# Scores in bursts of three head pairs, with a shared exponential, in a graph attention stack

## Chip, cores and metric

One core of a Trainium2 chip runs the whole program. The metric is the device time of one execution in microseconds. A core has five engines that run beside one another and wait for each other by semaphores: TensorE (PE; its weight loads are listed as PEld), VectorE (DVE), ScalarE (ACT), GpSimd (POOL) and SyncE (SP, which issues the DMAs here). Matmuls write PSUM, which has 8 banks of 128 partitions x 512 float32.

## What is computed

Sixteen graphs of 1024 nodes with 128 features share one adjacency matrix. Each goes through three transformer layers with masked attention, and then through one graph attention layer:

```python
# layers 0, 1, 2 (8 heads of 16)
Q, K, V = h @ Wq, h @ Wk, h @ Wv              # split into heads
scores = einsum('bnhd,bmhd->bhnm', Q, K) / sqrt(16)
scores = where(adj == 0, -inf, scores)
attn = softmax(scores, axis=-1)
x = layer_norm(h + einsum('bhnm,bmhd->bnhd', attn, V) @ Wo + bo)
x = layer_norm(x + relu(x @ W1 + b1) @ W2 + b2)
# layer 3
h = x @ W;  s_i = h @ a_src;  s_j = h @ a_dst
e = leaky_relu(s_i[:, :, None] + s_j[:, None, :], 0.2)
att = softmax(where(adj == 0, -inf, e))
out = layer_norm(einsum('bij,bjd->bid', att, h) + x)
```

Everything is float32. The softmax runs without subtracting a maximum; sums come from a column of ones beside V, and a check of their range at the end chooses a general path that isn't taken here.

## The kernel before

**Blocks and steps.** A block is one layer of one graph: 16 x 3 = 48 blocks, ordered in groups of four graphs (`blocks`). A block has 32 steps `(m, g, qh, kt)`: head group g (the heads are taken as four of each of two groups), half of the queries qh (512), tile of 128 keys kt. A step covers four heads, which are two pairs (`pp` 0 and 1).

**Scores** (`score_step`, L415 to L437). For each pair two matmuls with 64-row operands (L423, the rows hold high and low parts of q or k) fill a PSUM `slot()` of two banks; there are three slots, tag `s`. A pair is masked in one of two ways. On POOL: ACT takes the exponential from PSUM into the step's tile `e` (L430) and POOL multiplies by a 0/1 mask in place (L431). On DVE: DVE adds 0 or -57344 while it moves the scores from PSUM to `e` (L433), and ACT takes the exponential in place later (`exponentials`, L445). Pair 0 goes to POOL except at kt 2, 5 and 7 (`BOTH_ON_DVE`); pair 1 goes to DVE always. The 0/1 mask `mask01` has two bytes an element, the added one `mask_add` one byte.

**Products** (`av_step`, L447). Four steps later (`AHEAD`) eight matmul instructions multiply the four heads' exponentials by V into the accumulator bank `acc` (L450), 32 columns of the array for each head. After eight key tiles `finish` (L461 to L464) transposes the accumulator on DVE and divides.

**Pieces.** Everything else is cut into tasks that a planner puts between the steps: `piece()` runs at most one due task of the `chains` after each step's products. `AT` and `AT_END` give a step within the block for each task of `proj` (transposes, k and q with their high and low parts, v; L357 to L397) and `post` (output projection, norms, feed-forward; L469 to L529). `need()` forces a task that must be done. The last layer's tasks (`last_tasks`) follow gaps instead. A piece's matmuls use the one bank `t` (`bank()`), and ACT or DVE empties it. `split` casts the bank to the high part on ACT (L385) and subtracts it on DVE (L386). `edges(u)` makes 1024 x 256 edge weights: for each of two slots four matmuls (L607) and one DVE operation with `mask01` (L610), into a tile of the `e` pool; `aggregate(u)` multiplies them by the node features. `two(f, g)` runs an edge task and an aggregation as one piece.

**Stacking.** `stack(m, g)` copies the high and low parts of k and q into 64-row form, with 16 DMAs from SP for each group (L408). Group 1 is put down at step 1 of the block, and the next block's group 0 at step 21, after `need(("proj", m + 1))`.

**Order.** PE and ACT follow program order (`manual_schedule`). DVE and POOL follow the planner of the language, where `soon()` raises a priority, except at the start. Steps 1 to 4 also build the masks of the last four adjacency rows (`FIRST`).

**Tiles.** The `e` pool has 6 tiles of 128 x 4 x 512 float32; at the start they hold the first adjacency rows too.

Of the kernel before, what the change touches and what calls it, by code (L numbers as in the profile page):

```python
# [12 lines left out]
I32 = mybir.dt.int32  # L13
# [14 lines left out]
NEG_SLOPE = 0.2  # L28
SOON = 120
LANES = 4  # L30
FIRST = 1


AT = {"proj": (3, 6, 9, 11, 14, 15, 19, 20), "post": (12, 22, 23, 25, 26, 27, 28, 30, 32, 40, 41)}
AT_END = {3: (12, 21, 22, 24, 25, 26, 27, 28, 30, 31), 2: (8, 9, 13, 14, 15, 16, 17, 18, 20, 21)}
AHEAD = 4
BOTH_ON_DVE = (2, 5, 7)
TILES = {"w": 10, "x": LANES + 1, "last": 2}
BLOCKED = -57344.0

# [75 lines left out]
def fast_path(ctx: ExitStack, tc: tile.TileContext, a: dict, out: bass.AP, flag):  # L116
# [13 lines left out]
    def slot(dtype=F32):  # L130

        return psum.tile([P, N], dtype, tag="s", name="s", bufs=3)

    def bank():

        if head[0] or tail[0]:
            return slot()[:, :512]
        return psum.tile([P, 512], F32, tag="t", name="t", bufs=1)
# [5 lines left out]
        return work.tile([P, 512], F32, tag="w", name=name, bufs=TILES["w"])  # L144

    def e_tile():
        return work.tile([P, J, 512], F32, tag="e", name="e", bufs=6)


    def load_x(b):  # L150
# [25 lines left out]
    chk = const.tile([P, 2, B * (L + 1)], F32)  # L176


    mask01 = const.tile([P, NT, N], BF16)
    mask_add = const.tile([P, NT, N], F8W)  # L180
    rows_in = []
    for t in range(NT):
        if t < 6:
            ai = work.tile([P, 2, N], I32, tag="e", name="ai", bufs=6)
            ai, ab = ai[:, 0], ai.bitcast(BF16)[:, 1, :N]
        else:
            ai = work.tile([P, N], I32, tag="Wk", name="ai", bufs=4)
            ab = work.tile([P, N], BF16, tag="Wq", name="ab", bufs=4)
        rows_in.append((ai, ab))
# [15 lines left out]

    def masks(t, ps):
        psv = ps.rearrange("p (k q) -> p k q", q=P)
        nc.vector.tensor_copy(mask01[:, :, t * P:(t + 1) * P], psv)
        nc.scalar.activation(mask_add[:, :, t * P:(t + 1) * P], psv, AF.Identity, scale=-BLOCKED, bias=blocked,
                             saturate=False)  # L210

# [13 lines left out]
    def first_weights():  # L225
        W[0].update(load_layer(nc, nc.sync, const, a, 0, ("Wo", "b2", "W1", "b1", "W2", "ln1_g", "ln2_g")))
        norm_weights(nc.sync, 0)
# [184 lines left out]

    def score_step(step):  # L415
        m, g, qh, kt = step
        e = e_tile()
        q0 = qh * 512
        for pp in range(2):
            q, k = state["Wq", g, pp], state["Wk", g, pp]  # L420
            ps = slot()
            for r in range(2):
                nc.tensor.matmul(ps[:, r * 512:(r + 1) * 512], k[64 * r:64 * r + 64, kt * P:(kt + 1) * P],  # L423
                                 q[64 * r:64 * r + 64, q0:q0 + 512], start=True, stop=True)
            ev = e[:, 2 * pp:2 * pp + 2, :]
            psv = ps.rearrange("p (r q) -> p r q", q=512)
            on_pool = pp == 0 and kt not in BOTH_ON_DVE
            m = (mask01 if on_pool else mask_add)[:, kt, q0:q0 + 512][:, None, :].to_broadcast([P, 2, 512])
            if on_pool:
                nc.scalar.activation(ev, psv, AF.Exp, scale=HD ** -0.5)  # L430
                behind["pool"] = nc.gpsimd.tensor_mul(ev, ev, m).ins  # L431
            else:
                behind["dve"] = nc.vector.tensor_add(ev, psv, m).ins  # L433
                masked.append((2 * step_no[0] + pp + (kt not in BOTH_ON_DVE), ev))
        step_no[0] += 1
        exponentials()
        return e  # L437

    masked, step_no = [], [0]

    def exponentials(n=None):

        while masked and (n is not None or masked[0][0] < 2 * step_no[0] - 1):
            _, ev = masked.pop(0)
            nc.scalar.activation(ev, ev, AF.Exp, scale=HD ** -0.5)  # L445

    def av_step(step, e, acc, first, last):  # L447
        m, g, qh, kt = step
        for j in range(J):
            nc.tensor.matmul(acc[j * SLOT:j * SLOT + HD + 1, :], v_bufs[m % 2][:, kt, 2 * j + g, :], e[:, j, :],  # L450
                             start=first, stop=last)

    def finish(g, qh, acc):

# [80 lines left out]

    g_rows = const.tile([P, N], F32R)
    h_rows = const.tile([P, 512], F32R)

    def last_tasks(b):
# [54 lines left out]


        def edges(u):
            def run():
                e = s["e", u] = e_tile().rearrange("p j (c q) -> p (j c) q", q=256)  # L600
                for c in range(2):

                    ps = slot()
                    for i in range(2):
                        for r in range(2):
                            row = slice(64 * r + g0, 64 * r + g0 + 4)
                            nc.tensor.matmul(ps[:, (2 * r + i) * 256:(2 * r + i + 1) * 256],  # L607
                                             h_rows[row, (2 * i + c) * P:(2 * i + c + 1) * P],
                                             g_rows[row, u * 256:(u + 1) * 256], start=True, stop=True)
                    nc.vector.scalar_tensor_tensor(e[:, c:NT:2, :], ps.rearrange("p (j q) -> p j q", q=256), 1.0,  # L610
                                                   mask01[:, c:NT:2, u * 256:(u + 1) * 256], op0=OP.max, op1=OP.mult)
            return run

        def aggregate(u):
            def run():
                e, ps = s["e", u], bank()
                for i in range(2):
                    for t in range(NT):
# [21 lines left out]

        def two(f, g):
            def run():
                f()
                g()
            return run

        return [(5, xt(0), "+w +last +w +w"), (1, xt(1), "+w"), (2, nodes(0, 3), ""), (2, nodes(3, 6), ""), (2, nodes(6, 8), "-w -w"),
# [78 lines left out]

    def av_due(n):

        for item in [w for w in waiting if w[2] <= n]:
            step, e, _ = item  # L730
            half = step[:3]
            if half not in accs:
                if accs:
# [2 lines left out]
                left[half] = NT  # L736
            waiting.remove(item)
            left[half] -= 1
            av_step(step, e, accs[half], left[half] == NT - 1, left[half] == 0)
            if left[half]:  # L740
                continue
            m, g, qh = half
# [16 lines left out]
                if l == L - 1:  # L759
                    put(last_tasks(b), ("last", b), chain)  # L760

    n = 0
    with tc.manual_schedule(engines={mybir.EngineType.PE, mybir.EngineType.Activation}):
        for m, (b, l) in enumerate(blocks):
            order = [(g, qh) for g in range(G) for qh in range(2)]
            if m in (0, len(blocks) - 1):
                order.sort(key=lambda x: x[1])
            for at, (g, qh, kt) in enumerate((g, qh, kt) for g, qh in order for kt in range(NT)):
                now[0] = n
                if at == (6 if m == 0 else 1):  # L770
                    stack(m, 1)
                if n == 6:
                    with tc.issue_after(behind["stack"]):
                        first_weights()
                        other_weights()
                if n == 20:
                    with tc.issue_after(behind["pool"]):
                        biases()
                if n == 40:
                    with tc.issue_after(behind["dve"]):  # L780
                        last_weights()
                if at == 0 and m + 2 < len(blocks) and blocks[m + 2][1] == 0:
                    put([(0, fetch(blocks[m + 2][0]), "+x")], ("fetch", blocks[m + 2][0]))
                if m + 1 < len(blocks):
                    if at == (6 if m == 0 else 0):
                        need(("post",) + (blocks[m + 1][0], blocks[m + 1][1] - 1) if blocks[m + 1][1] else
                             ("fetch", blocks[m + 1][0]))
                        put(proj_tasks(m + 1), ("proj", m + 1), first=True)
                    if at == (24 if m == 0 else 21):
                        need(("proj", m + 1))  # L790
                        stack(m + 1, 0)
                step = m, g, qh, kt
                if FIRST <= n < FIRST + 4:

                    with tc.manual_schedule(engines={mybir.EngineType.DVE}):
                        e = score_step(step)
                        neighbours(4 + n - FIRST)
                        masks(4 + n - FIRST, mask_rows(4 + n - FIRST))
                else:
                    e = score_step(step)  # L800
                waiting.append((step, e, n + AHEAD))
                av_due(n)
                piece()
                n += 1
        exponentials(0)
        for n in range(n, n + 2 * AHEAD):
            now[0] = n
            av_due(n)
            piece()
        tail[0] = True  # L810
        while chains:
            now[0] += 1
            for chain in list(chains):
                if is_due(chain):
                    take(chain)
# [236 lines left out]
```

## Time and profile before

| | us |
|---|---|
| median of 3 runs (lowest, highest) | 3996.08 (3995.59, 3997.26) |
| the profiled execution | 3992.41 |
| its span, first to last instruction | 3990.6 |
| ACT exponentials from PSUM, L430, x960 | 983.6 busy, 1025 ns each |
| PE products, L450, x12288 | 1632.5 busy, 603 ns each |
| PE scores, L423, x6144 | 1175.0 busy, 455 ns each |
| DVE edge operation, L610, x128 | 150.3 busy, 1213 ns each |
| POOL layer norm scale, L345, 128x1024, x95 | 227.5 busy, 2395 ns each |

The mean granted TensorE clock is 0.985. A group's busy time is the union of its instructions' spans. Matmuls overlap, so on PE the distance from start to start says more than the duration; on ACT and DVE, too, an instruction starts some 0.1 us before its predecessor's span ends. The last column of a group's line is the idle time of the engine before it, and what ended most of it. In the timeline, consecutive instructions of one line are merged.

### The profile page before, as it was taken

The numbers are of one execution on the slowest core, as the hardware profiler recorded it, in microseconds if no ns is written. First come the engines' busy times: TensorE is split into PE (matmuls) and PEld (weight loads), VectorE is DVE, ScalarE is ACT, GpSimd is POOL, SyncE is SP. The second block draws the span as 40 slices with busy tenths as digits, with TensorE's granted clock in tenths as the row PEclk, the third lists the DMA queues.
The fourth block names the chain that finished last, engine by engine and source line by source line (L and its number), as shares of the span: only waits on it lengthen the run. The fifth ranks groups of instructions, "written<-read, shape, count | busy, mean of one in ns | idle before, by whom it ended". The sixth has DMA issues, their size and how long they took to land.

```text
span 3990.6 us, 107765 instructions
## 1 busy us (share of the span) xinstructions
PE 3758.4 (94%) x44501; PEld 1550.6 (39%) x44501; DVE 3410.8 (85%) x5326; ACT 3380.6 (85%) x3961; POOL 3454.8 (87%) x3010
## 2 busy tenths in 40 slices
PE   7999999999999999999999999999999999999996
PEld 2333333344443333334444333333444433333345
DVE  7888988988888988988788898888888898898874
ACT  7999999977779999997777999999777799999860
POOL 5889989988889999998888998999888898998975
PEclk8999999999999999999999999999999999999998
DMA  6222222112222222222222222221222212222200
GB/s 162 64 65 55 53 65 65 48 44 75 55 55 52 65 65 55 53 65 55 55 55 55 65 57 52 65 65 46 57 52 55 65 48 65 64 52 56 65 8 20
DMA packets 124464, 233.12 MB, mean 58 GB/s; under 512 B 34624, under 2 KB 73792, under 8 KB 123968
## 3 DMA queue, kind: packets, MB, share of 16 engines
q1 hardware_dynamic: 123056, 225.74, 22.6%
q8 instruction: 354, 5.80, 0.6%
q14 instruction: 142, 1.16, 0.1%
q10 hardware_dynamic: 912, 0.42, 0.0%
HBM read 15.54 MB, written 8.39 MB: 6 GB/s over the span
## 4 chain that ended last, share of the span: by engine, by line
PE 60%; DVE 18%; POOL 14%; issue 4%; ACT 3%; SPq 0%; DMA 0%; DVEq 0%; POOLq 0%; ACTq 0%
PE acc L450 23%; PE t L297 18%; PE s L423 15%; DVE e L433 10%; POOL e L431 7%; POOL x L345 3%; POOL x L346 3%; DVE st L322 3%; PE t L286 2%; DVE x L329 1%; POOL mv L339 1%; ACT e L445 1%; DVE lo L386 1%; PE s L297 1%; DVE mv L324 1%
## 5 line engine op out<-in xcount | busy, mean ns | idle before, releaser
L433 DVE TENSOR_TENSOR e<-s,mask_add 128x1024 f32<-128x1024 f32 x2112 | 2492.2, 1213 | 320.0 <-PE s L423 242.8
L445 ACT ACTIVATE e<-e 128x1024 f32<-128x1024 f32 x2112 | 2194.3, 1062 | 197.0 <-DVE e L433 181.8
L431 POOL TENSOR_TENSOR e<-e,mask 128x1024 f32<-128x1024 f32 x960 | 2055.1, 2155 | 326.3 <-ACT e L430 306.2
L450 PE MATMUL acc<-e,v 128*17 128x512 f32 x12288 | 1632.5, 603 | 56.4 <-POOL e L431 25.2
L423 PE MATMUL s<-Wq,Wk 64*128 64x512 f32 x6144 | 1175.0, 455 | 52.3 <-DVE e L433 35.1
L430 ACT ACTIVATE e<-s 128x1024 f32<-128x1024 f32 x960 | 983.6, 1025 | 241.6 <-PE s L423 241.5
L423 PEld LDWEIGHTS s<-Wq,Wk 64*128 64x128 f32 x6144 | 498.9, 185 | 1009.6 <-issue 396.2
L450 PEld LDWEIGHTS acc<-e,v 128*17 128x17 f32 x12288 | 208.0, 95 | 565.6 <-issue 464.4
L341 POOL TENSOR_SCALAR x<-x,mv 128x128 f32<-128x128 f32 x896 | 392.0, 453 | 23.5
L339 POOL TENSOR_TENSOR mv<-mv,half_neg 128x4 f32<-128x4 f32 x224 | 232.7, 1039 | 18.7
L345 POOL TENSOR_TENSOR x<-x,ln_g 128x1024 f32<-128x1024 f32 (+1 forms) x97 | 230.0, 2372 | 11.7 <-PE t L286 6.1
L297 PE MATMUL t<-hd,e 128*32 128x129 f32 x7040 | 207.8, 275 | 1.2
L329 DVE TENSOR_TENSOR x<-t,x 128x512 f32<-128x512 f32 x191 | 130.8, 685 | 85.6 <-PE t L297 85.6
L322 DVE BATCH_NORM_STATS2 st<-x 128x6 f32<-128x128 f32 x896 | 197.2, 279 | 3.3
L297 PEld LDWEIGHTS t<-hd,e 128*32 128x32 f32 x7040 | 193.5, 110 | 16.7 <-DVE lo L386 9.9
L297 PE MATMUL t<-x1T,W 128*32 128x512 f32 x1520 | 198.0, 592 | 0.0
L297 PEld LDWEIGHTS t<-W,hT 128*32 128x32 f32 x6080 | 169.9, 110 | 58.5 <-issue 45.2
L297 PE MATMUL t<-W,hT 128*32 128x128 f32 x6080 | 183.4, 273 | 0.2 <-DVE x L625 0.2
L286 PEld LDWEIGHTS t<-identf,x 128*128 128x128 f32 x872 | 93.8, 141 | 221.7 <-issue 81.8
L286 PE MATMUL t<-identf,x 128*128 128x128 f32 x872 | 153.7, 291 | 21.7 <-DVE hd L575 7.1
L386 DVE TENSOR_TENSOR lo<-t,hi 128x512 fp32r<-128x512 f32 x188 | 128.2, 682 | 35.6 <-ACT hi L385 35.6
L610 DVE SCALAR_TENSOR_TENSOR e<-s,mask 128x1024 f32<-128x1024 f32 x128 | 150.3, 1213 | 6.1 <-PE s L607 5.4
(118 smaller groups left out, 2493.9 us busy)
## 6 DMA issues: line engine op xcount, KB each, us to landing
Wk<-hi SPq DMA_DIRECT2D x384, 128.0 KB
Wk<-lo SPq DMA_DIRECT2D x384, 128.0 KB
Wq<-hi SPq DMA_DIRECT2D x384, 128.0 KB
Wq<-lo SPq DMA_DIRECT2D x384, 128.0 KB
x<-in_x_dram SPq DMA_DIRECT2D x16, 512.0 KB
out_dram<-x SPq DMA_DIRECT2D x31, 256.0 KB
ai<-in_adj_dram SPq DMA_DIRECT2D x8, 512.0 KB
g_rows<-parts SPq DMA_DIRECT2D x124, 4.0 KB
```

Of the source, the lines that this page charges most:

```text
L286: nc.tensor.transpose(ps[:, t * P:(t + 1) * P], src[:, 4 * h + t, :], identf)
L297: nc.tensor.matmul(dst[j:j + SLOT, :], lhsT[:, j:j + SLOT], rhs, start=start, stop=stop)
L322: nc.vector.bn_stats(st[:, t, :], z[:, t, :])
L339: nc.gpsimd.tensor_tensor(v, v, half_neg[:, ts], OP.pow)
L341: nc.gpsimd.tensor_scalar(z[:, t, :], z[:, t, :], mv[:, t, 0:1], mv[:, t, 1:2], op0=OP.add, op1=OP.mult)
L345: nc.gpsimd.tensor_mul(z, z, rows(gain, n))
L423: nc.tensor.matmul(ps[:, r * 512:(r + 1) * 512], k[64 * r:64 * r + 64, kt * P:(kt + 1) * P], q[64 * r:64 * r + 64, q0:q0 + 512], start=Tru ...
L430: nc.scalar.activation(ev, psv, AF.Exp, scale=HD ** -0.5)
L431: behind["pool"] = nc.gpsimd.tensor_mul(ev, ev, m).ins
L433: behind["dve"] = nc.vector.tensor_add(ev, psv, m).ins
L445: nc.scalar.activation(ev, ev, AF.Exp, scale=HD ** -0.5)
L450: nc.tensor.matmul(acc[j * SLOT:j * SLOT + HD + 1, :], v_bufs[m % 2][:, kt, 2 * j + g, :], e[:, j, :], start=first, stop=last)
```

## The change

- Scores are issued in bursts of three pairs, that is one and a half steps, whatever step a pair belongs to. In a burst, pairs 1 and 3 are masked on DVE into the two halves of one `e` tile, and pair 2 on POOL into a tile of a new pool `ep`. In every 16th burst pair 2 goes to DVE too. The DVE pairs of a burst share one exponential of 128 x 2048, which ACT runs in the next burst.
- After a burst's scores come the products and pieces of the steps that it completed, one or two in turn. Where it completed two, the exponentials come first, then products, piece, products, piece. Where one or none, a piece comes first, then the exponentials, then products and a piece.
- An edge task no longer computes at once: it queues its fill, and the next burst is the fill and one pair, on POOL. `two` runs the aggregation first.
- `mask01` has one byte an element. The `e` pool has 5 tiles, `ep` 4 of 128 x 2 x 512.
- The second q piece of `proj` moves from step 15 to 17.
- The masks of the last four rows are built in the first four bursts.

```diff
-FIRST = 1
-AT = {"proj": (3, 6, 9, 11, 14, 15, 19, 20), "post": (12, 22, 23, 25, 26, 27, 28, 30, 32, 40, 41)}
+AT = {"proj": (3, 6, 9, 11, 14, 17, 19, 20), "post": (12, 22, 23, 25, 26, 27, 28, 30, 32, 40, 41)}
-BOTH_ON_DVE = (2, 5, 7)
+BURST = 3
+POOL_RESTS = 16
+E_TILES = {"e": 5, "ep": 4}
...
-    mask01 = const.tile([P, NT, N], BF16)
+    mask01 = const.tile([P, NT, N], F8W)
...
+    def on_dve(step, pp, ev):
+        psv = scores(step, pp)
+        behind["dve"] = nc.vector.tensor_add(ev, psv, mask_of(mask_add, step)).ins
+        e_of.setdefault(step, {})[pp] = ev
+
+    def on_pool(step, pp, ev):
+        psv = scores(step, pp)
+        nc.scalar.activation(ev, psv, AF.Exp, scale=HD ** -0.5)
+        behind["pool"] = nc.gpsimd.tensor_mul(ev, ev, mask_of(mask01, step)).ins
+        e_of.setdefault(step, {})[pp] = ev
+
+    e_of, masked, bursts = {}, [], [0]
+
+    def burst(edge, pairs):
+        old = list(masked)
+        masked.clear()
+        if edge is not None:
+            edge()
+            on_pool(*pairs[0], e_pair())
+        else:
+            e, ep = e_tile(), e_pair()
+            rests = bursts[0] % POOL_RESTS == POOL_RESTS - 1 or len(pairs) < BURST
+            for i, pair in enumerate(pairs):
+                if i == 1:
+                    (on_dve if rests else on_pool)(*pair, ep)
+                else:
+                    on_dve(*pair, e[:, i:i + 2, :])
+            masked.append(e[:, 0:2 * ((len(pairs) + 1) // 2)])
+            if rests and len(pairs) > 1:
+                masked.append(ep)
+            bursts[0] += 1
+        return old
+
+    def exponentials(evs):
+        for ev in evs:
             nc.scalar.activation(ev, ev, AF.Exp, scale=HD ** -0.5)
...
+            def run():
+                extra.append(fill)
+                if tail[0]:
+                    flush()
             return run
 
         def aggregate(u):
             def run():
+                if ("e", u) not in s:
+                    flush()
...
+        while p < 2 * len(steps):
+            edge = extra.popleft() if extra else None
+            take_n = 1 if edge else min(BURST, 2 * len(steps) - p)
+            pairs = []
+            for i in range(p, p + take_n):
+                if i % 2 == 0:
+                    before(i // 2)
+                pairs.append((steps[i // 2], i % 2))
...
+            p += take_n
+            ready = range(full, p // 2)
+            full = p // 2
+            for n in ready:
+                waiting.append((steps[n], n + AHEAD))
+            if len(ready) == 2:
+                exponentials(old)
+                av_due(ready[0])
+                at_step(ready[0], piece)
+                av_due(ready[1])
+                at_step(ready[1], piece)
+            else:
+                n = p // 2 - 1
+                at_step(n, piece)
+                exponentials(old)
+                if ready:
+                    av_due(n)
+                    at_step(n, piece)
```

`scores(step, pp)` holds the two matmuls and the slot of the old `score_step`, `mask_of` the broadcast slice of a mask, and `before(n)` the stacking, loads and task entries that the old loop ran ahead of a step. `av_step` takes each pair's exponentials from where its burst put them.

More of the change, by code (lines that the diff above doesn't have):

```diff
@@ L146, in e_tile, with e_pair @@
     def e_tile():
-        return work.tile([P, J, 512], F32, tag="e", name="e", bufs=6)
+        return work.tile([P, J, 512], F32, tag="e", name="e", bufs=E_TILES["e"])
+    def e_pair():
+        return work.tile([P, 2, 512], F32, tag="ep", name="e", bufs=E_TILES["ep"])
     def load_x(b):
@@ L182, in fast_path @@
     for t in range(NT):
-        if t < 6:
-            ai = work.tile([P, 2, N], I32, tag="e", name="ai", bufs=6)
+        if t < E_TILES["e"]:
+            ai = work.tile([P, 2, N], I32, tag="e", name="ai", bufs=E_TILES["e"])
             ai, ab = ai[:, 0], ai.bitcast(BF16)[:, 1, :N]
+        elif t < 6:
+            ai = work.tile([P, N], I32, tag="ep", name="ai", bufs=E_TILES["ep"])
+            ab = work.tile([P, N], BF16, tag="ep", name="ab", bufs=E_TILES["ep"])
         else:
@@ L207, in masks @@
         psv = ps.rearrange("p (k q) -> p k q", q=P)
-        nc.vector.tensor_copy(mask01[:, :, t * P:(t + 1) * P], psv)
+        nc.vector.tensor_copy(mask01[:, :, t * P:(t + 1) * P], psv, saturate=False)
         nc.scalar.activation(mask_add[:, :, t * P:(t + 1) * P], psv, AF.Identity, scale=-BLOCKED, bias=blocked,
@@ L409, in stack, with scores @@
                 state[n, g, pp] = t
-    def score_step(step):
+    def scores(step, pp):
         m, g, qh, kt = step
[L417 to L444, printed above, removed]
+        q, k = state["Wq", g, pp], state["Wk", g, pp]
+        ps = slot()
+        for r in range(2):
+            nc.tensor.matmul(ps[:, r * 512:(r + 1) * 512], k[64 * r:64 * r + 64, kt * P:(kt + 1) * P],
+                             q[64 * r:64 * r + 64, qh * 512:(qh + 1) * 512], start=True, stop=True)
+        return ps.rearrange("p (r q) -> p r q", q=512)
@@ new lines, in mask_of @@
+    def mask_of(mask, step):
+        _, _, qh, kt = step
+        return mask[:, kt, qh * 512:(qh + 1) * 512][:, None, :].to_broadcast([P, 2, 512])
+    def on_dve(step, pp, ev):
[7 more added lines that the diff above has]
+        e_of.setdefault(step, {})[pp] = ev
@@ L445, in exponentials, with av_step @@
+    def exponentials(evs):
+        for ev in evs:
             nc.scalar.activation(ev, ev, AF.Exp, scale=HD ** -0.5)
-    def av_step(step, e, acc, first, last):
+    def av_step(step, acc, first, last):
         m, g, qh, kt = step
+        e = e_of.pop(step)
         for j in range(J):
-            nc.tensor.matmul(acc[j * SLOT:j * SLOT + HD + 1, :], v_bufs[m % 2][:, kt, 2 * j + g, :], e[:, j, :],
-                             start=first, stop=last)
+            nc.tensor.matmul(acc[j * SLOT:j * SLOT + HD + 1, :], v_bufs[m % 2][:, kt, 2 * j + g, :],
+                             e[j // 2][:, j % 2, :], start=first, stop=last)
@@ L529, in post_tasks, with flush @@
         return together, alone
+    extra = deque()
+    def flush():
+        while extra:
+            extra.popleft()()
     g_rows = const.tile([P, N], F32R)
@@ L598, in edges, with fill @@
         def edges(u):
-            def run():
+            def fill():
                 e = s["e", u] = e_tile().rearrange("p j (c q) -> p (j c) q", q=256)
@@ L642, in run @@
             def run():
+                g()
                 f()
-                g()
             return run
@@ L727, in av_due @@
     def av_due(n):
-        for item in [w for w in waiting if w[2] <= n]:
-            step, e, _ = item
+        now[0] = n
+        for item in [w for w in waiting if w[1] <= n]:
+            step, _ = item
             half = step[:3]
@@ L738, in av_due @@
             left[half] -= 1
-            av_step(step, e, accs[half], left[half] == NT - 1, left[half] == 0)
+            av_step(step, accs[half], left[half] == NT - 1, left[half] == 0)
             if left[half]:
@@ L760, in av_due @@
                     put(last_tasks(b), ("last", b), chain)
-    n = 0
-    with tc.manual_schedule(engines={mybir.EngineType.PE, mybir.EngineType.Activation}):
[L764 to L805, printed above, removed]
@@ new lines, in fast_path, with before @@
+    steps = []
+    for m in range(len(blocks)):
+        order = [(g, qh) for g in range(G) for qh in range(2)]
+        if m in (0, len(blocks) - 1):
+            order.sort(key=lambda x: x[1])
+        steps += [(m, g, qh, kt) for g, qh in order for kt in range(NT)]
+    def before(n):
+        m, at = n // (4 * NT), n % (4 * NT)
+        now[0] = n
+        if at == (6 if m == 0 else 1):
+            stack(m, 1)
+        if n == 6:
+            with tc.issue_after(behind["stack"]):
+                first_weights()
+                other_weights()
+        if n == 20:
+            with tc.issue_after(behind["pool"]):
+                biases()
+        if n == 40:
+            with tc.issue_after(behind["dve"]):
+                last_weights()
+        if at == 0 and m + 2 < len(blocks) and blocks[m + 2][1] == 0:
+            put([(0, fetch(blocks[m + 2][0]), "+x")], ("fetch", blocks[m + 2][0]))
+        if m + 1 < len(blocks):
+            if at == (6 if m == 0 else 0):
+                need(("post",) + (blocks[m + 1][0], blocks[m + 1][1] - 1) if blocks[m + 1][1] else
+                     ("fetch", blocks[m + 1][0]))
+                put(proj_tasks(m + 1), ("proj", m + 1), first=True)
+            if at == (24 if m == 0 else 21):
+                need(("proj", m + 1))
+                stack(m + 1, 0)
@@ new lines, in at_step @@
+    def at_step(n, f):
+        now[0] = n
+        f()
+    late = deque(range(4, NT))
+    full = 0
+    with tc.manual_schedule(engines={mybir.EngineType.PE, mybir.EngineType.Activation}):
+        p = 0
+        while p < 2 * len(steps):
[6 more added lines that the diff above has]
+                pairs.append((steps[i // 2], i % 2))
+            if late:
+                with tc.manual_schedule(engines={mybir.EngineType.DVE}):
+                    old = burst(edge, pairs)
+                    t = late.popleft()
+                    neighbours(t)
+                    masks(t, mask_rows(t))
+            else:
+                old = burst(edge, pairs)
+            p += take_n
[9 more added lines that the diff above has]
+                at_step(ready[1], piece)
+            else:
+                n = p // 2 - 1
[4 more added lines that the diff above has]
+                    at_step(n, piece)
+        exponentials(masked)
+        n = len(steps)
```

## The prediction

> **What bounds the kernel now.** I read, in this order, the busy shares, the chain of work that ended last, the costly groups, engine totals by stretch, and PE's timeline.
>
> ```profile
> PE 3758.4 (94%) x44501; PEld 1550.6 (39%) x44501; DVE 3410.8 (85%) x5326; ACT 3380.6 (85%) x3961; POOL 3454.8 (87%) x3010
> ...
> PE 60%; DVE 18%; POOL 14%; issue 4%; ACT 3%; SPq 0%; DMA 0%; DVEq 0%; POOLq 0%; ACTq 0%
> ...
> L433 DVE TENSOR_TENSOR e<-s,mask_add 128x1024 f32<-128x1024 f32 x2112 | 2492.2, 1213 | 320.0 <-PE s L423 242.8
> L445 ACT ACTIVATE e<-e 128x1024 f32<-128x1024 f32 x2112 | 2194.3, 1062 | 197.0 <-DVE e L433 181.8
> L431 POOL TENSOR_TENSOR e<-e,mask 128x1024 f32<-128x1024 f32 x960 | 2055.1, 2155 | 326.3 <-ACT e L430 306.2
> ```
>
> PE is the first limit, with three engines close behind. The four accumulator transposes of each block (L461) cut the run into 48 blocks: 30 of them take 73.2 us each and hold no task of the last layer; the others take 79 to 110. The engine totals of one regular block and one long block (stretch and length, then busy PE, PEld, DVE, ACT, POOL, with instruction counts):
>
> ```profile
> 1527.40:1600.60 73.20, 70.39 (x722) 25.76 (x720) 65.39 (x97) 69.12 (x79) 67.25 (x57) 1.00 0.23 59
> 2021.30:2120.90 99.60, 92.03 (x1337) 44.38 (x1337) 81.37 (x140) 72.56 (x92) 81.17 (x76) 0.98 0.21 54
> ```
>
> In a regular block POOL has only 6 us to spare and DVE 8, so PE's gains are worth their face value only until one of those is reached. In the long block PE alone is near its limit. Now PE's timeline (start, duration, group):
>
> ```profile
> 1576.88 0.73 PE L423 MATMUL s<-Wq,Wk 64*128 64x512 f32 x4
> 1577.54 1.05 PE L450 MATMUL acc<-e,v 128*17 128x512 f32 x8
> 1578.41 1.04 PE L297 MATMUL t<-x1T,W 128*32 128x512 f32 x8
> 1579.38 0.73 PE L423 MATMUL s<-Wq,Wk 64*128 64x512 f32 x4
> ```
>
> Start to start: two score pairs 0.66, a step's products 0.87, a piece of the same shape as the products (8 matmuls of 512 columns) 0.97 when scores follow. So entering the scores costs 0.10 to 0.11. And inside the scores? Two pairs take 0.33 each. The only place where more than two pairs of the same row-split kind run in a row is the last layer's edges, 256 columns wide; these lines are from three stretches, each starting one pair later:
>
> ```profile
> 952.71 0.75 PE L607 MATMUL s<-g_rows,h_rows 4*128 4x256 f32 x8
> ...
> 952.93 0.53 PE L607 MATMUL s<-g_rows,h_rows 4*128 4x256 f32 x6
> ...
> 953.05 0.41 PE L607 MATMUL s<-g_rows,h_rows 4*128 4x256 f32 x4
> ```
>
> First to second pair 0.22, second to third 0.12: the first weight load (0.10) lies open, later ones hide behind the stream. Last, a stall in every block, in the two q pieces of consecutive steps:
>
> ```profile
> 1550.95 1.04 PE L297 MATMUL t<-xT,Wq 128*32 128x512 f32 x8
> 1551.92 0.73 PE L423 MATMUL s<-Wq,Wk 64*128 64x512 f32 x4
> 1552.58 1.05 PE L450 MATMUL acc<-e,v 128*17 128x512 f32 x8
> 1554.76 1.06 PE L297 MATMUL t<-xT,Wq 128*32 128x512 f32 x8 [1.12 <-DVE lo L386]
> ```
>
> 2.18 us from products to piece instead of 0.87: the one `t` bank was still held by the first q piece, whose subtraction stood behind three mask additions on DVE. Loss 1.31 us.
>
> **Scores in threes.** Before, 1.5 steps cost PE 1.5 x (0.11 + 0.66) = 1.155 us of scores and entries. After, a burst pays one entry, two pairs at 0.33 and a third. The trace has no third pair of 512 columns. Upper bound: 0.33, like the others. Lower: twice the edges' 0.12, so 0.24. I take 0.24, since those matmuls also reuse the same row groups with new weights. Burst: 0.11 + 0.66 + 0.24 = 1.01; saved 0.145 (0.055 at the upper bound). Of 3072 pairs 60 go alone behind an edge fill (15 graphs x 4; the last graph's edges fall in the tail), so there are 3012 / 3 = 1004 bursts: -146 us (-55). The 60 lone pairs share the edges' entry: 60 x 0.11 = -7.
>
> The Trainium skill (TensorE: Matmul & The Clock Gate, Part 3, what overlaps) speaks against this: weight loads overlap running matmuls only when the row group differs, and pairs 1, 2 and 3 use the same two. By that rule the third pair would cost 0.33 and the term would be -55. The edge rows, same row groups, show 0.12 after 0.22, so the measurement decides.
>
> **Who handles which pair.** Pairs 1 and 3 go to DVE, pair 2 to POOL except in each 16th burst. A regular block of 64 pairs is 21.3 bursts: 20.0 pairs on POOL, 44.0 on DVE, and before it was 20 and 44. So POOL stays at 67.3 and DVE at 65.4 per block; they become the next limits. The lone edge pairs add 42 POOL pairs to the whole run (1002 against 960), 42 x 2.155 = 90 us, all in long blocks, where POOL has 18 of 99.6 us idle: cost nothing there; uncovered, 90.
>
> **One-byte 0/1 mask on POOL.** No POOL row has a one-byte operand. With a float32 second operand the same size takes 2395 ns (L345), with the two-byte mask 2155. Bounds: 2395, and 2035 if bytes set the difference (240 ns for two bytes, 120 for one). I take 2155, the nearest row; on DVE the byte mask (L433) and the two-byte mask (L610) both cost 1213. The edges' DVE operation therefore costs the same, as do the eight mask copies at the start.
>
> **The shared exponential.** 1062 ns each, and the next starts 0.95 later. An instruction of 512 columns takes 582 (L385), one of 1024 from PSUM 1025: 0.87 ns a column, so the second 1024 of a wide one cost 0.89 to 0.95 us, and a merge saves 0 to 0.06; 21.3 merges, 0 to 1.3 us a block on ACT, off the path. ACT keeps 4 us of room. Price: whatever stands behind the wide one waits 1.84 instead of 0.95.
>
> **The q piece from step 15 to 17** removes the 1.31: 47 projections, -61 us; by the idle time alone (1.12) -53. I take -53. Bounds: nothing, if the bank is late anyway. Its stack of DMAs moves too: in this block SP issued the Wk and Wq copies from 1552 to 1564, held for q's cast; two steps later they end near 1569, needed at the next block's first scores near 1591. Covered; 16 issues of 0.6 us, 10 us, would show only if that were gone. The next group's SP copies wait for the block's last scores anyway.
>
> **A new wait: two pieces in one burst.** A burst that completes two steps runs products, piece, products, piece. Between those pieces lies only 0.87 us instead of 0.87 + 0.66 + 0.11, while the first piece's evacuation stands on ACT behind POOL's exponential and the wide one: 0.55 (pair 2 ready) + 0.91 + 1.84 + 0.70 = 4.0 after the burst's start, against PE at the second piece at 0.11 + 0.90 + 0.87 + 0.97 + 0.87 = 3.7. With latency I take 0.5 us; bounds 0 and 1.0 (short pieces, or DVE evacuating). The step tables hold 7 adjacent PE pieces, a third fall in one burst: 2.3 x 0.5 = 1.2 us a block, +56 (0 to +108). Behind the waiting piece stand the next burst's scores, so DVE and ACT run dry by as much.
>
> **What DVE won't give.** In the first part of the block (1527.4 to 1553.9) DVE is busy 25.78 of 26.50 us. Its work there stays, so of PE's 12 steps' saving (8 bursts x 0.145 = 1.16) only about 0.7 can appear: 0.45 x 47 = +21.
>
> **Buffers.** A burst's tile is free three bursts later; five and four are there, so no wait. POOL's product deadline stays about 10 us after the scores.
>
> **Sum** against this execution's span, 3990.6: -146 - 7 - 53 + 56 + 21 = -129, span 3861.6. The execution's own time is 3992.41 and the median of the runs 3996.08, 5.5 above the span: 3867. A regular block then takes 70.4, above POOL's 67.3. The likeliest case's own range: third pair at 0.33, +91, to no piece waits and no DVE toll, -77: 3790 to 3958.
>
> **Rivals.**
> *POOL paces regular blocks.* Its busy 67.3 plus idle it can't use, since it is fed by the current exponentials: 3.1 of its 5.9 idle is waiting for L430, the rest small gaps. If half of the remaining 2.8 also stays, 71.8; then 30 x -1.4 = -42 and 17 long blocks x -2.7 = -46: 3996 - 88 = 3908. For: POOL's gaps come in the light steps, where it can't work ahead. Against: faster PE feeds it sooner. 0.18.
> *Everything hides:* -146 - 7 - 61, no new wait: 3782. Against: DVE full in a third of the block. 0.09.
> *Slower: the third score blocks the products.* In program order the products stand behind pair 3, whose slot comes free only after both DVE additions (2 x 1.14) and any DVE work queued between. With a statistics piece (0.65 + 4 x 0.2 + 4 x 0.07 = 1.7) that is 4.0 after the evacuation starts at 0.6, so 4.6, while PE is there at 1.01 + 1.30 of products + 0.6 of piece + 0.77 = 3.7: 0.9 us idle with finished exponentials unused. With 4 statistics and 2 split pieces a block, 6 x 0.9 = 5.4 x 47 = +254 on -129: 4121. It decides from 129 / 47 / 6 = 0.46 us each. For: DVE is the chain's second engine (18%). Against: before, too, each pair waits for the pair three earlier, and such waits are already in the 73.2. 0.13.
> *Slower: POOL's byte mask at 2395:* 20 x 0.24 = 4.8 on 67.3 and 3.1 idle gives 75.2 in regular blocks, +2.0 x 30, less 46: about 4010; slower from 2.37 us on. 0.07.
> Forecast 0.53.
>
> **Numbers.** 0.2% (8 us) is about what a measurement can tell from no change. Faster: forecast, POOL pacing and all hidden: 0.79 of 0.80; slower 0.18; same 0.03. The range holds the forecast, POOL pacing and the POOL-price case, and part of the others: 3790 to 4015.
>
> **What would show it.** Right: PE's timeline with L423 groups of six in about 0.90 us to the next group; no wait of `xT,Wq` pieces for `lo`; regular blocks near 70.4; L431's successor at 2155 with 1002 instances. Wrong: third pair 0.33 after the second; POOL rows above 2.37 us; score loads waiting over 0.46 us per heavy burst for DVE; a piece waiting for ACT in most bursts.

## The result, and the profile after

The changed kernel takes 4394.74 us (median of 4 runs, 4392.37 to 4396.74) against 3996.67 for the kernel before on the same chip: a ratio of 1.100, 95% interval 1.0986 to 1.1017. Forecast were 3867 us and a gain. 398 us were lost. One of the four runs of `steps` below took 12333 us, the only slow run of all; it is left out of that kernel's ratio, and why it was slow stays open.

The page of the changed kernel, first its engines (busy, share, instructions), then its three large groups beside PE (busy, mean ns | idle before, releaser):

```profile
PE 3790.1 (86%) x44501; PEld 1623.3 (37%) x44501; DVE 3370.9 (77%) x5288; ACT 3303.8 (75%) x2955; POOL 3408.4 (78%) x3048
...
L438 DVE TENSOR_TENSOR e<-s,mask_add 128x1024 f32<-128x1024 f32 x2074 | 2425.2, 1214 | 493.2 <-PE s L428 484.0
L444 POOL TENSOR_TENSOR e<-e,mask 128x1024 f32<-128x1024 f32 x998 | 2010.0, 2023 | 617.6 <-ACT e L443 610.8
L473 ACT ACTIVATE e<-e 128x2048 f32<-128x2048 f32 x1068 | 1976.6, 1861 | 5.6 <-DVE e L438 5.6
```

No engine got more work: PE has the same 44501 matmuls (busy for 32 us more), DVE, ACT and POOL are busy for 40 to 77 us less than before, and each of these three is idle for over 950 us. So the time went into waits. DVE waited 484 us for scores (243 before). Now the waits in the other direction, PE for DVE (in all, times, longest), of the changed kernel:

```profile
PEld s L428 <- DVE e L438: 519.4, 615, 2.0
...
PE s L428 <- DVE e L438: 153.4, 226, 1.6
```

And of the kernel before:

```profile
PEld s L423 <- DVE e L433: 338.0, 469, 1.7
...
PE s L423 <- DVE e L433: 35.1, 83, 0.9
```

PE and DVE wait for each other in turn. PE's timeline shows how (start, duration, group, idle before it):

```profile
2563.19 0.74 PE L428 MATMUL s<-Wq,Wk 64*128 64x512 f32 x4
2564.27 0.50 PE L428 MATMUL s<-Wq,Wk 64*128 64x512 f32 x2 [0.34 <-DVE e L438]
2564.70 1.91 PE L479 MATMUL acc<-e,v 128*17 128x512 f32 x16
2566.43 1.06 PE L304 MATMUL t<-Wo,aT 128*32 128x128 f32 x32
2567.41 0.96 PE L428 MATMUL s<-Wq,Wk 64*128 64x512 f32 x6
2568.31 0.66 PE L293 MATMUL t<-identf,x 128*128 128x128 f32 x4
2568.89 1.05 PE L479 MATMUL acc<-e,v 128*17 128x512 f32 x8
2569.88 0.73 PE L428 MATMUL s<-Wq,Wk 64*128 64x512 f32 x4
2571.59 0.50 PE L428 MATMUL s<-Wq,Wk 64*128 64x512 f32 x2 [0.99 <-DVE e L438]
```

And DVE in the same stretch:

```profile
2561.86 4.62 DVE L438 TENSOR_TENSOR e<-s,mask_add 128x1024 f32<-128x1024 f32 x4 [2.52 <-PE s L428]
2567.55 0.69 DVE L336 TENSOR_TENSOR x<-t,x 128x512 f32<-128x512 f32 x1 [1.07 <-PE t L304]
2568.16 1.22 DVE L438 TENSOR_TENSOR e<-s,mask_add 128x1024 f32<-128x1024 f32 x1
```

Where the slots are free, six matmuls leave together and the next group starts 0.90 us later (2567.41 to 2568.31), as forecast. But the burst at 2563.19 gets only two pairs out at once: its third stands 0.34 us for a slot that DVE hasn't emptied. Then come 2.7 us of two steps of products and a piece, in which DVE empties all slots and falls idle for 1.07 us. The next burst has one step of products, its successor follows after 2.5 us, and pair 3 waits again, 0.99 us, with 16 products behind it.

To sum such waits over the run, the following table takes the distance between the starts of neighbouring groups on PE (a score pair, the eight products of a step, a piece), less what is usual for the same two lines and the same size of the first group: the 10th percentile. A second score pair usually follows the first after 0.335 us, in all kernels, and a third follows the second after 0.231. "First pairs" are those behind products or pieces. "Into products" counts from scores, pieces and products. The few distances around edge fills are left out. The blocks are cut as in the prediction; "regular" are the same 30, "long" 16 others. All us.

| kernel | median | between score pairs | first pairs | into pieces | into products | regular block | long block |
|---|---|---|---|---|---|---|---|
| before | 3997 | 64 | 38 | 103 | 93 | 73.2 | 92.6 |
| changed | 4395 | 318 | 59 | 298 | 147 | 78.6 | 104.6 |
| b3_single | 4370 | 310 | 61 | 302 | 136 | 79.4 | 102.2 |
| third_later | 4332 | 96 | 117 | 331 | 100 | 77.4 | 103.5 |
| pair3_off_dve | 4286 | 229 | 72 | 345 | 91 | 75.4 | 104.4 |
| steps | 4098 | 88 | 68 | 126 | 88 | 73.9 | 95.8 |
| kt_early_exp | 4069 | 98 | 52 | 85 | 116 | 73.5 | 95.3 |
| before_2slots | 4617 | 520 | 119 | 120 | 107 | 86.7 | 103.8 |
| q17_and_mask | 3981 | 69 | 48 | 61 | 117 | 73.2 | 91.9 |

The expectations below give 426 us between score pairs for the changed kernel. That sum counts a second pair, too, from 0.23 us on, so that 105 us of it are no wait; other waits that they name (92, 147) also differ somewhat from this table's count.

The table accounts for the loss. Together with the distances left out, the waits rise by 537 us; the shorter scores take back some 146 by the prediction's own term, which leaves 391 of the 398. In the 30 regular blocks alone they rise by 8.6 us a block: 4.6 between score pairs, 2.2 into pieces, 1.2 into products, 0.5 at first pairs. The shorter scores take back 3.1 (21.3 x 0.145), and the block grew by 5.4.

### The profile page after: what moved, and what is told of

The parts are those of the page before. It is cut to its first block, busy times and chain, and to the rows that moved or that the text cites. A ratio compares the mean times of both kernels' runs of the same rounds, so it can differ in the third digit from the quotient of the medians.

```text
span 4393.5 us, 106698 instructions
## 1 busy us (share of the span) xinstructions
PE 3790.1 (86%) x44501; PEld 1623.3 (37%) x44501; DVE 3370.9 (77%) x5288; ACT 3303.8 (75%) x2955; POOL 3408.4 (78%) x3048
## 5 line engine op out<-in xcount | busy, mean ns | idle before, releaser
L438 DVE TENSOR_TENSOR e<-s,mask_add 128x1024 f32<-128x1024 f32 x2074 | 2425.2, 1214 | 493.2 <-PE s L428 484.0
L444 POOL TENSOR_TENSOR e<-e,mask 128x1024 f32<-128x1024 f32 x998 | 2010.0, 2023 | 617.6 <-ACT e L443 610.8
L473 ACT ACTIVATE e<-e 128x2048 f32<-128x2048 f32 x1068 | 1976.6, 1861 | 5.6 <-DVE e L438 5.6
L443 ACT ACTIVATE e<-s 128x1024 f32<-128x1024 f32 x998 | 1021.1, 1023 | 590.0 <-PE s L428 316.4
L428 PE MATMUL s<-Wq,Wk 64*128 64x512 f32 x6144 | 1119.8, 448 | 240.6 <-DVE e L438 153.4
L479 PEld LDWEIGHTS acc<-e,v 128*17 128x17 f32 x12288 | 276.6, 97 | 625.6 <-issue 483.8
L352 POOL TENSOR_TENSOR x<-x,ln_g 128x1024 f32<-128x1024 f32 x97 | 229.3, 2364 | 17.0 <-PE t L293 16.3
L344 POOL TENSOR_SCALAR mv<-mv 128x4 f32<-128x4 f32 x224 | 52.9, 236 | 222.3 <-DVE mv L331 180.8
L490 DVE STREAM_TRANSPOSE tt<-acc 128x512 f32<-128x512 f32 x192 | 136.9, 713 | 64.7 <-PE acc L479 57.4
L535 ACT ACTIVATE hT<-t,b 128x512 f32<-128x512 f32 x190 | 130.5, 687 | 70.2 <-PE t L304 70.1
```

The costliest lines, as they stand in the source:

```text
L352: nc.gpsimd.tensor_mul(z, z, rows(gain, n))
L438: behind["dve"] = nc.vector.tensor_add(ev, psv, mask_of(mask_add, step)).ins
L444: behind["pool"] = nc.gpsimd.tensor_mul(ev, ev, mask_of(mask01, step)).ins
```

## The experiments

**Bursts of one step** (`steps`). Each pair gets a tile and an exponential of its own, still every third pair goes to POOL (`i` counts the pairs), and each burst has at most one piece, behind its products. Everything else of the change stays.

```diff
-BURST = 3
-E_TILES = {"e": 5, "ep": 4}
+BURST = 2
+E_TILES = {"e": 1, "ep": 12}
...
+            for pair in pairs:
+                ev = e_pair()
...
+                if i % 3 == 1 and i // 3 % POOL_RESTS != POOL_RESTS - 1:
+                    on_pool(*pair, ev)
+                else:
+                    on_dve(*pair, ev)
+                    masked.append(ev)
```

> The changed kernel with bursts of two pairs, one step, products of one step and one piece after each; everything else of the change stays: a third of the pairs on POOL, the one-byte mask, the queued edge fills, the q piece at 17. Each pair has its own tile and its own exponential. Theory A (uneven bursts: three slots are filled at once, short bursts outrun DVE, long ones let it run dry, and two pieces meet in one burst): the loss goes away, 3900 to 3990 us, score-to-score waits on PE back to about 65 us from 426. Theory B (the loss lies in the shares, the mask or the edge fills): it stays above 4200.

4098 us, ratio 1.0253 (1.0232 to 1.0273). The waits between score pairs go from 318 to 88 us and those into pieces from 298 to 126. Its waits of PE for DVE:

```profile
PEld s L428 <- DVE e L438: 258.6, 337, 1.9
...
PE s L428 <- DVE e L438: 29.3, 57, 1.7
```

The time misses the range of theory A, but three quarters of the loss are gone; 101 us remain.

**Bursts of three, single exponentials** (`b3_single`): the same tiles, bursts of three.

> The changed kernel, bursts of three, but each pair has its own tile and its own exponential of 1024 columns instead of one of 2048 for two pairs. Theory A: the wide exponential is not the cause, within 60 us of 4395. Theory C (the wide exponential holds up ACT and the pieces behind it): 4395 falls by 150 or more.

4370 us (1.094; 1.0922 to 1.0959), 25 below the changed kernel: the wide exponential isn't the cause. Against `steps`, which differs in the burst and the order of products and pieces that goes with it, 272 us: the price of the burst, with that order. (The lower clock, told of at the end, can account for at most 66 of them: b3_single has 288 us at half clock, `steps` 156.) The waits of ACT for products (228 us in the changed kernel) are gone here, for there are twelve pair tiles; the long blocks gain 2.4 us each by it, the regular ones lose 0.8.

**Edge fill alone** (`edge_alone`).

```diff
-            take_n = 1 if edge else min(BURST, 2 * len(steps) - p)
+            take_n = 0 if edge else min(BURST, 2 * len(steps) - p)
```

> The changed kernel, with an edge fill as a burst of its own, without the one pair on POOL. In the long blocks ACT waited 228 us, 79 times, for products to free the tile of POOL's pair. Theory D (the lone pair takes a tile of a pool of four that was sized for bursts of three pairs, and ACT stands still with all that is behind it): those waits vanish and 16 long blocks gain 5 us or more each, 4300 or below. Theory A alone: the long blocks change by less than 2 us each, 4365 to 4425.

4436 us (1.1099; 1.108 to 1.1117), slower by 41. The waits of ACT for a tile vanish and the long blocks still grow, to 107.1. Theory D falls. Why it got slower isn't shown: the edit also moves 38 pairs from POOL to DVE (960 and 2112 instead of 998 and 2074), and the waits between score pairs rise to 358.

**Pieces balanced** (`balanced`): without the piece between two products. **One piece per burst** (`one_piece`): also without the early piece of a short burst.

```diff
                 exponentials(old)
                 av_due(ready[0])
-                at_step(ready[0], piece)
                 av_due(ready[1])
...
```

> The changed kernel, where a burst that completes two steps runs products, products, piece, and no piece between them; a piece that is due then goes to the next, short burst, ahead of its exponentials. Theory A: short bursts grow longer and long ones shorter, so PE waits less for slots and for the one bank: 4150 to 4300. Rival E (what counts is the total of DVE's work per burst, not how even the bursts are): within 60 us of 4395.

> The changed kernel with at most one piece per burst, always after its products: products, products, piece or products, piece. In regular blocks 19 pieces meet 21.3 bursts, so none is forced. Theory G (two pieces with only 0.87 us between them wait on the one bank t): PE's waits at pieces fall from 147 us in the 30 regular blocks to under 60, and a regular block from 78.6 to 75.5 or less. Rival: those waits are DVE's and ACT's lateness after the uneven scores, and stay: over 120 us, 78 or more per block.

4366 (1.0923; 1.0904 to 1.0941) and 4292 us (1.0754; 1.0738 to 1.0771). Theories A and G both miss, and `balanced` ends where rival E put it: taking a piece out of the long bursts is worth 28 us. The waits into pieces of the 30 regular blocks are 105 and 85 us against 111 in the changed kernel. `one_piece` never has two pieces in a burst, so a short distance between two pieces is not the main thing that they wait for. `one_piece` gains 102 us in all, but it also shifts pieces of the long blocks into regular ones (81.1 and 92.7 us), so its blocks can't be compared one by one, and why it gains stays open.

**Pair 3 behind the first products** (`third_later`).

```diff
                 exponentials(old)
                 av_due(ready[0])
+                last_pair()
                 at_step(ready[0], piece)
...
```

> The changed kernel with pair 3 of a burst behind the first products instead of before them. PE pays a second entry into the scores and an open weight load per burst, 0.21 us x 1004 = 211 us of PE time at most. Theory A1 (products that are ready stand behind a third pair whose slot DVE hasn't emptied): PE's score-to-score waits fall from 426 to under 250 us and the time falls in spite of the added entries, 4250 to 4360. Rival: the waits are short enough to be paid anyway, and the entries come on top, 4450 or more.

4332 us (1.0844; 1.0824 to 1.0864). The waits between score pairs fall from 318 to 96 us, as A1 has it. A part comes back at first pairs, 59 to 117, where the moved pair now counts, and into pieces, 298 to 331. The run gains 62 us although PE enters the scores twice in a burst. So products that could run did stand behind the third pair.

**Pair 3 without DVE** (`pair3_off_dve`). This kernel leaves out the mask of pair 3, so its output is not the program's; only its time counts.

```diff
...
-                    on_dve(*pair, e[:, i:i + 2, :])
+                    psv = scores(*pair)
+                    nc.scalar.activation(e[:, 2:4, :], psv, AF.Exp, scale=HD ** -0.5)
...
```

> The changed kernel with pair 3 not masked at all (its mask is left out, which also takes 1004 DVE additions of 1.14 us away): ACT takes its exponential straight from PSUM; pair 1 has an exponential of its own. ACT's work stays within 80 us. Theory A1 (DVE's two additions per burst hold the slots): score-to-score waits fall from 426 to under 150 us, and the time to 4000 to 4150. Rival F (the order of products and pieces and the one bank are the loss, whatever empties the slots): 4280 or more.

4286 us (1.072; 1.0703 to 1.0736), 109 less, but short of A1's figure and just inside rival F's. DVE is busy for only 53%. In regular blocks the waits between score pairs fall from 169 to 79 us, and the block from 78.6 to 75.4: 3.2 of the 5.4 us lost. There DVE's emptying of the slots is the larger part. In long blocks nothing is gained (104.6 to 104.4); over the whole run 229 us between score pairs stay, now for ACT as well, and the waits into pieces rise by 47. So DVE's pace is one part, and the order of products and pieces may be another; no run separates them fully.

**Two slots in the kernel before** (`before_2slots`): there a step of two pairs then uses every slot.

```diff
-        return psum.tile([P, N], dtype, tag="s", name="s", bufs=3)
+        return psum.tile([P, N], dtype, tag="s", name="s", bufs=2)
```

> The kernel before with two PSUM slots instead of three, so that a step of two pairs uses all of them, as a burst of three uses all three. Theory H (a burst that uses every slot leaves none in reserve, so PE waits at each burst's start or end for DVE or ACT): score-to-score and score waits rise from 92 us to 350 or more and the time to 4250 or more. Rival (one spare slot is worth little, it is the uneven products that hurt): under 4120.

4617 us (1.1561; 1.1543 to 1.1579). Its waits of PE:

```profile
PEld s L423 <- DVE e L433: 924.8, 1065, 2.0
...
PEld s L423 <- ACT e L430: 347.6, 343, 2.0
...
PE s L423 <- DVE e L433: 332.5, 615, 1.7
```

Waits at and between score pairs rise from 102 us to 639, with the same instructions on every engine, and DVE's waits for scores to 602. Theory H holds: in this kernel a step of two pairs needs a slot beyond its own. The matching test, a burst of three with a fourth slot, has no run: three slots of two banks, `acc` and `t` take all 8 banks.

**The small edits alone**: the q piece at 17 (`q17_alone`), the one-byte mask (`mask_alone`), both (`q17_and_mask`); then both with a 2048-column exponential at key tiles 2, 5 and 7 (`before_merged`).

> The kernel before with only the second q piece moved from step 15 to 17. The prediction's term: 47 x 1.12 = 53 us less, 3935 to 3950. Rival: the wait goes elsewhere (the two v pieces follow at 19 and 20, DVE's backlog stays), 3985 to 3997.

> The kernel before with only the 0/1 mask in one byte. The changed kernel's POOL rows show 2023 ns where before had 2155. Theory: POOL gets 960 x 0.13 = 127 us of idle time and no end moves, 3975 to 3997. Rival: POOL's waits were on the path more than its 14% of the chain suggests, 3960 or below.

> The kernel before with the q piece at 17 and the one-byte mask, without the merged exponentials that made it 4075. Theory L (a wide exponential holds up the piece evacuations behind it on ACT): 3975 to 3992, so the merges cost some 85. Rival (the two small edits together cost it): 4030 or more.

> The kernel before with the q piece at 17, the one-byte mask, and one exponential of 2048 columns at key tiles 2, 5 and 7, where both pairs are on DVE (576 merges). Neither of the first two moved the time alone, the regular block stayed at 73.17. Theory I (ACT, 94% busy, and DVE pace the regular block): a merge saves ACT 0.09 us, 12 a block, so up to 1.1 us a block, 3940 to 3980. Rival (nothing in this block hangs on ACT's total): within 8 us of 3990.

Ratios in this order: 0.9995 (0.9986 to 1.0004), 0.9982 (0.9973 to 0.9991), 0.9962 (0.9948 to 0.9975; 3980.8 us, the fastest kernel of this study) and 1.0202 (1.0188 to 1.0216). Theory I falls: the merge takes ACT's busy time from 3392 to 3332 us and costs 94 us of the run, as theory L has it. Waits into pieces more than double, 61 to 143. In the merged kernel a row of PE's weight loads waiting for an evacuation reads

```profile
PEld t L297 <- ACT hT L509: 72.5, 119, 0.9
```

where the kernel without merges has 42.3 for the same 119.

**What is left of `steps`**: the old share of pairs (`steps_kt`), that with edges at once (`steps_kt_direct`; `steps_direct` is the same on `steps`), with the old order of exponentials (`kt_early_exp`), and with two edge tiles and ten pair tiles (`kt_early_exp_tiles`).

```diff
-                if i % 3 == 1 and i // 3 % POOL_RESTS != POOL_RESTS - 1:
+                if pair[1] == 0 and pair[0][3] not in (2, 5, 7):
...
-                    masked.append(ev)
+                    (old if pair[1] == 0 else masked).append(ev)
```

> The kernel with bursts of one step (4098), and the edge task computing at once, inside its piece, as before the change, instead of being queued for the next burst. Theory: the queued fills with their lone pair are what makes the long blocks 3.3 us longer than before (95.8 against 92.6); they return to within 1 us of 92.6 and the time to about 4045. Rival: the new split of the pairs over the steps does it, less than 15 us change.

> The kernel with bursts of one step (4098), and the pairs shared out as before the change: pair 0 to POOL except at key tiles 2, 5 and 7. The rest of the change stays (one-byte mask, q piece at 17, queued edge fills, a tile for each pair). Theory J (giving every third pair to POOL, whichever place it has in its step, is the 100 us that bursts of one step still lose: POOL's pair comes second in half of the steps, behind DVE's): back to 3930 to 3990, faster than both kernels if the queued fills keep the 52 us that they were worth at one step. Rival K (the tile pools and the order of aggregation and fill): 4060 or more.

> The same with the edge task computing at once, after the aggregation. It differs from the kernel before in the one-byte mask, the q piece, a tile for each pair and that order. Theory J: 3980 to 4000, as before; Rival K: 4080 or more.

> Bursts of one step, the old share of pairs, and the old order of exponentials too: where both pairs of a step are on DVE, the first one's exponential follows in the same burst instead of in the next one, so that ACT never has three in a row ahead of a piece's evacuation. Theory M (the order of exponentials is what the one-step kernels lose in regular blocks, 74.36 against 73.2): a regular block back to within 0.3 of 73.2 us, 4045 to 4065 in all. Rival N (the tile pools): no change, 4080 or more.

> The same with two large tiles for edge fills instead of one, and ten for pairs instead of twelve. Theory N (with one tile an edge fill waits for the aggregation of the last one, in the long blocks alone): long blocks from 94.6 to 93 or less, 20 to 40 us in all below the run beside it. Rival: ten tiles for pairs leave no reserve for four steps of lead, and regular blocks lose 1 us or more each.

`steps_direct` takes 4150 us (1.0394): the queued fills were worth 52 us, the opposite of what was expected. `steps_kt` 4091 (1.0236; 1.0222 to 1.025): theory J falls, the share of pairs is worth 7 us at most, which is within the noise. `steps_kt_direct` 4150 (1.0384). `kt_early_exp` 4069 (1.0181; 1.0164 to 1.0198), its regular block 73.5: theory M holds for 22 us. `kt_early_exp_tiles` 4065 (1.0171; 1.0154 to 1.0188): the tiles don't matter.

The 398 us, from median to median, in the one order in which the runs take the change apart: bursts of three instead of one step, with their order of products and pieces, 272; the shared exponential with its tiles 25; the share of pairs 7; the order of exponentials 22; the rest, between `kt_early_exp` and `q17_and_mask`, 88 (54 of it in the 16 long blocks, 27 after the last block, so mostly the edge work); less 16 for the two small edits. What costs the 88 (the lone pair, the aggregation ahead of the fill, the tiles of pairs, the order at the start) wasn't separated.

## Why the prediction was wrong

**The third pair, -146: the mechanism was right.** Pair 3 follows pair 2 after 0.23 us, against 0.24 in the sum. The 0.33 that the prediction works out from the rule of the Trainium skill (TensorE: Matmul & The Clock Gate, Part 3, what overlaps) is not what the trace shows. Entering the scores behind products costs 0.10 us (0.97 to a score pair, 0.87 to further products), against 0.11 in the sum.

**"Before, too, each pair waits for the pair three earlier, and such waits are already in the 73.2": this step failed.** With it the prediction put the third pair's wait for a slot at nothing and its slower rival at a chance of 0.13. Before, a step fills two slots of three, and its first pair takes the one left over from the step before; PE lost 30 us at second pairs in the 30 regular blocks. A burst of three takes all slots at once. DVE needs 2 x 1.14 us for its two; a burst with one step of products lasts some 1.9 us (0.90 + 0.97, an estimate from the distances above), and PE waits; a burst with two steps and pieces lasts more than twice that (4.2 us from 2563.19 to 2567.41, 0.34 of them a wait), and DVE waits. Measured were 169 us at second and third pairs of the regular blocks, 139 more than before. Of the 640 third pairs in them 212 come over 0.05 us late, 7 a block, and all together lose 5.5 us a block: the rival had said 6 bursts with 0.9 us, 5.4. So the rival had the place and the price right, and only its chance was too low. Over the whole run the waits between score pairs rise by 254 us, exactly the rival's term; that is luck, for it is 4.6 in a regular block and more in the long ones. `before_2slots` shows what a slot in reserve is worth, and `steps` brings the waits back to 88 us, though with another order of products and pieces.

**Two pieces in a burst, +56: too small, and its cause isn't the main one.** Waits into pieces rise by 195 us, in regular blocks by 2.2 a block instead of 1.2, and `one_piece`, with never two pieces in a burst, keeps 85 of the 111 us of the regular blocks. With one step a burst they are 126 us. That ACT and DVE, fed in lumps, come late to the bank fits this but isn't shown. The rival's total, 4121, lacks these waits, and those into products, which no term had and which rise by 54 us.

**The q piece, -53: wrong.** It measured -0.05%, no change. The bank's stall went: PE's own waits at pieces for `lo` fall from 47.7 to 18.8 us, the waits into pieces in regular blocks from 44 to 4. But the block stayed at 73.2, with waits elsewhere: into products 45 to 68, at first pairs 19 to 31, between pairs 30 to 37. A likely reason stands in the prediction itself, though no run tests it: in this stretch DVE was busy for 25.78 of 26.50 us. The prediction charged that limit to the third pair and not to the q piece; both together could give 0.7 us.

**The shared exponential, "off the path": wrong.** A wide one takes 1.91 us, and what stands behind it waits. In the kernel before it costs 94 us at 576 merges; in the changed kernel 25 together with its few tiles.

**Buffers, "no wait": wrong, but cheap.** ACT waited 79 times, 228 us in all, for products to free a tile of POOL's pair. With twelve tiles and single exponentials these waits are gone, and the run gains 25 us.

**The one-byte mask at 2155: the lower bound, 2035, was right.** It is 2023 here and 2029 in `mask_alone`, and it brought 0.2%: POOL had idle time before as well.

**Pairs per engine and the edges.** 998 and 2074 instead of 1002 and 2070. POOL is busy for only 62.8 of 75.9 us in a regular block of the changed kernel (2524.53 to 2600.43). The edge bursts, taken for a small gain (-7), sit in blocks that grew by 12 us; 8.8 of these go with bursts of one step.

## What to carry to other kernels

Count how many buffers of a shared pool one burst takes, against all there are: here a burst that takes every one had no reserve, and producer and consumer then waited in turn although both had time to spare. When a sentence sets a slower rival aside, price that sentence too; the rival's own price stood in the prediction and was right. Before you book a stall on one engine as a gain, look at what the fullest engine of that stretch has idle; here a stall of 1.1 us a block was removed for nothing. Merging instructions on an engine that keeps program order saved 0.1 us a merge here, and whatever stands behind a merged one waits for its second half, too: the merges cost 94 us.

## What the runs showed that was not expected

The price of POOL's multiply depends on the width of the second operand: 2395 ns with four bytes (L345), 2155 with two, 2023 with one. The granted clock fell, too, from a mean of 0.985 to 0.969. The clock records of these traces hold only full and half, so that is 2 x 0.031 x 4393.5 = 272 us at half, against 120. In the changed kernel a regular block (2524.53 to 2600.43) has 1.00, a long one (1031.83 to 1144.93) 0.97. By an estimate from these sums it costs at most half of the difference, 76 of the 398 us. One stretch in that long block, with a granted clock of 0.62 from 1067.36 to 1071.80:

```profile
1067.36 1.54 PE L479 MATMUL acc<-e,v 128*17 128x512 f32 x8
1068.65 1.96 PE L304 MATMUL t<-xT,Wk 128*32 128x512 f32 x8
1070.36 1.47 PE L479 MATMUL acc<-e,v 128*17 128x512 f32 x8
```

The same groups take 1.05, 1.04 and 1.04 us elsewhere. Whether the waits bring the clock down isn't shown: `before_merged` takes 4075 us, 94 more than the same kernel without merges, at 0.988 against 0.987.
